# Zero products where no bank of sums is open: a graph layer on one Trainium2 core

## The chip, the cores and the metric

The kernel runs on one core of one Trainium2 chip. The core has five engines that run side by side, each through its own list of instructions in order: PE (TensorE, matmuls; its weight loads are shown as PEld), DVE (VectorE), ACT (ScalarE), POOL (GpSimd) and SP (SyncE, which here issues the transfers). Matmul results go into eight banks of PSUM, an accumulator memory that DVE and ACT read. The clock of TensorE can be granted at full speed (1.00) or less.

The metric is the device time of one execution in microseconds (us), lower is better. The time shown for a kernel is the median of its runs.

## The reference

Inputs are `x` (4096 x 64), an adjacency matrix `adj` (4096 x 4096, of 0.0 and 1.0 in float32, 64 MiB), a weight (64 x 64) and a bias (64). Cut to what is computed:

```python
h = relu(layernorm(x))
support = h @ weight
mask = adj != 0
rank = cumsum(mask, axis=1)             # how many neighbours up to here in the row
deg = rank[:, -1:]
k = minimum(deg, 100)
pos = rank - (deg - k)
w = mask * where(pos > 0, 0.5 ** (k - pos), 0)
out = x + w @ support + bias
```

For a neighbour, `k - pos` is the number of neighbours to its right in the same row. So each neighbour weighs one half to the power of that number, and only the last 100 neighbours of a row count. The work is to read 64 MiB, to count to the right in every row, to take a power and to multiply by `support`.

## The kernel before, in words

The adjacency matrix is cut into 32 tiles of 128 rows. Each tile passes through the same steps, each a small function of the kernel:

- `load` (SP, L355) brings a tile into one of four buffers `a_sb`. The first two and the last four tiles come in pieces. A buffer is free again once it is converted.
- `convert` (DVE, L563) makes bytes of the floats, and `flip` (DVE, L573) transposes in blocks of 32, so that a row's elements lie along the partitions (`mt`).
- `totals` (PE, L581) counts neighbours in blocks, into a bank. `split` (ACT, L589) takes two kinds of count out of it (`sums`). `suffix` (PE, L602) adds up the blocks to the right, into a bank. `clamp` (DVE, L608) cuts off what lies more than 100 neighbours away (`behind`).
- `place` (PE, L618 and L622) makes the count to the right of every element, into four banks at once. `weigh` (ACT, L636, four per tile) takes the power and writes the weights `wk`. In the last tiles DVE does some of this with `encode` and `take` (L643, L647).
- `aggregate` (PE, L656) multiplies the weights of two tiles with `support` (`hr`), in eight calls of four matmuls, into a part of a bank of sums. A bank of sums serves four tiles, except for the last four, whose two pairs have a bank each.
- `drain` (ACT or DVE, L671 and L673) takes a finished bank of sums and adds the bias. `turn_back` (PE, L679) transposes it back, `finish` (DVE, L685) adds `x`, and `store` (SP, L689) writes the result.

Layer norm, `support` and constants (L370 to L551) are made in the first 40 us, beside the first tiles.

**What sets the order.** All steps are made as tasks with a due time from a list written into the kernel. A function `plan` goes through them with estimated durations. It gives out the eight banks, and it returns one list of steps; every engine executes its own steps in the order of this list. For a step that needs new banks, `plan` names them, and they become the list `homes`, from which the step takes them with `bank()`. The banks 0 to 7 of the plan are called `bank` in the profile, and a step that takes a bank waits until its last reader is done with it.

**The zero products.** `plan` also returns with every step of PE a number `spare`. It estimates the time for which PE has nothing to do before the step and the matmul rows of the last 3.4 us, and from both works out how many products of zeros should be put in. The loop over the plan calls `warm(spare)` ahead of each step. `warm` (L482 to L484) makes that many matmuls of 128 x 256 zeros (`junk`). They go into the place that the list `idle` names: a bank and a column in it. At the start that is the second half of the last bank; after each `aggregate` it is the part of the bank of sums that this call added to. There the products have neither a first nor a last mark, so that zero is added to open sums. When `drain` takes that bank, `idle` is emptied. From then until the next `aggregate` in the list no bank of sums is open, and `warm` makes nothing, whatever `spare` says.

Of the kernel before, what the change touches and what calls it, by code (L numbers as in the profile page):

```python
# [118 lines left out]
def read_by(u):  # L119

    g = u // 2
    return [("drain", d) for d, (k, i0, i1, _) in enumerate(DRAINS) if k == g and (u not in ALONE or i0 == u % 2 * 2)][-1:]
# [102 lines left out]
def dma_ns(f, args):  # L225
    if f == "fetch":
        return 950
    _, k0, k1 = LOADS[args[0]]
    return (k1 - k0) * {8: 611, 4: 620, 2: 630}[k1 - k0] + (300 if args[0] == REST else 0)


def late(at):

    return 450 if at < 17000 else 1900 if at < 104000 else 3300


def rows_of(f, args):

    return {"turn": 150, "center": 2048, "support": 2048, "totals": 512, "suffix": 1408, "place": 1024, "aggregate": 1024,
            "turn_back": 2048}.get(f, 0)  # L240


def plan():

    todo, kinds = tasks(), {}
    for key, (f, args, engine, *_) in todo.items():
        kinds.setdefault((engine, f), []).append(key)
    ready, free = {None: 0}, list(FREE)
    landed, taken, order = 0, {p: [] for p in SIZES}, []
    banks = [None] * (BANKS - 1) + read_by(0)  # L250
    while kinds:
        heads = []
        for kind, keys in kinds.items():
            f, args, engine, due, hold, lag, needs, pool = todo[keys[0]]
            if pool and pool[0] in SIZES:
                needs = needs + (taken[pool[0]] + list(pool[1:]))[:-SIZES[pool[0]]][-len(pool) + 1:]
            elif pool:
                needs = needs + [k for _, _, k in sorted((ready[k], i, k) for i, k in enumerate(banks) if k in ready)][:len(pool) - 1]
                if len(needs) < len(todo[keys[0]][6]) + len(pool) - 1:
                    continue  # L260
            if all(r in ready for r in needs):
                heads.append((max([free[engine]] + [ready[r] for r in needs]), due, engine, kind))
        soon, _, engine, _ = min(heads)
        _, at, kind = min((due, at, kind) for at, due, e, kind in heads if e == engine and at <= soon + WAIT[engine])
        key = kinds[kind].pop(0)
        if not kinds[kind]:
            del kinds[kind]
        f, args, _, _, hold, lag, _, pool = todo[key]
        homes = []
        if pool and pool[0] in SIZES:  # L270
            taken[pool[0]] += pool[1:]
        elif pool:
            homes = [i for _, i in sorted((ready[k], i) for i, k in enumerate(banks) if k in ready)][:len(pool) - 1]
            for i, k in zip(homes, pool[1:]):
                banks[i] = k
        if f in ("load", "fetch"):
            lag = max(landed - at, 2450) + dma_ns(f, args)
            landed = at + lag
            lag += late(landed)
        if f in FULL:  # L280
            hold, lag = hold + 95, lag + 95
        ready[key] = at + lag + 60
        free[engine] = at + hold
        order.append((at, hold, engine, f, args, homes))
    spent, end, result = [], 1200, []
    for at, hold, engine, f, args, homes in order:
        idle = 0
        if engine == PE:
            recent = sum(rows for when, rows in spent if when > at - 3400)
            idle = max(0, min(int((at - end) * 0.6) // 110, (4200 - recent) // 256))  # L290
            spent += [(at, rows_of(f, args) + 256 * idle)]
            end = at + hold
        result.append((at, idle, f, args, homes))
    return result
# [3 lines left out]
def kernel(  # L298
# [12 lines left out]
    nc = tc.nc  # L311
    P = 128
# [21 lines left out]
    banks = [ps.tile([P, W], F32, name=f"bank{i}") for i in range(BANKS)]  # L334
    homes = []
# [35 lines left out]
    junk = setup.tile([P, 2 * P], BF16, name="junk")  # L371
# [108 lines left out]
    idle = [banks[BANKS - 1], 2 * P]  # L480

    def warm(n):  # L482
        for i in range(n if idle else 0):
            nc.tensor.matmul(idle[0][:, idle[1]:idle[1] + 2 * P], junk[:, :P], junk, start=not accs, stop=not accs, skip_group_check=True)  # L484

    pxs, ns = {}, {}

# [68 lines left out]
    masks, words, wts, accs, pts, sums8, behind, vs, codes = {}, {}, {}, {}, {}, {}, {}, {}, {}  # L556
# [130 lines left out]
    def store(s):  # L687
# [5 lines left out]
        support, scale, first, second, convert, flip, totals, split, suffix, clamp, place, weigh, encode, take, aggregate,  # L693
        drain, turn_back, finish, store)}
    for at, spare, f, args, given in plan():
        warm(spare)
        homes[:] = given
        does[f](*args)

    last = {}  # L700
# [34 lines left out]
```

## Time and profile before

| | |
|---|---|
| runs of the kernel | 185.85, 186.7 and 187.02 us; median 186.7 |
| profiled execution | 187.01 us, of which its span 185.0 us (first to last instruction) |
| PE, weight loads | 165.2 us busy (89%), 128.4 us (69%); 2087 matmuls |
| DVE | 153.9 us busy (83%) |
| ACT | 149.5 us busy (81%) |
| POOL | 7.7 us busy (4%) |
| mean granted clock of TensorE | 0.980 |
| DMA | 69.55 MB, 376 GB/s over the span |
| zero products (L484) | 93, 14.7 us busy, mean 299 ns |
| first reading of the matrix | loads (L355) issued from 1.2 to 150.9 us |

Busy time is the time in which an engine has an instruction running. Matmuls overlap: a mean of 299 ns for one does not mean that the next starts 299 ns later. In the view of 40 slices each digit is the busy share of 4.6 us in tenths, 9 for 90% or more; the row PEclk shows the granted clock in the same way. An idle time in brackets in the timeline names what the engine waited for. A wait for several things is put down to the one that came last.

### The profile page before, as it was taken

How to read it: one execution, taken by the hardware profiler on the slowest of the kernel's cores; microseconds unless marked ns; L12 is line 12 of the kernel's file. 1: busy time of each engine (PE TensorE's matmuls, PEld its weight loads, DVE VectorE, ACT ScalarE, POOL GpSimd, SP SyncE). 2: the span in 40 equal slices, each digit the busy share in tenths (PEclk: the TensorE clock that was granted, in tenths of full speed). 3: DMA queues.
4: the chain of work that ended last, by engine and by line, in shares of the span. 5: the costliest groups of instructions: out<-in, count | busy, mean ns of one | idle time of the engine just before them, and what ended most of it. 6: DMA issues, size and time to landing. Idle time of an engine off the chain costs nothing.

```text
span 185.0 us, 4842 instructions
## 1 busy us (share of the span) xinstructions
PE 165.2 (89%) x2087; PEld 128.4 (69%) x2087; DVE 153.9 (83%) x204; ACT 149.5 (81%) x196; POOL 7.7 (4%) x43
## 2 busy tenths in 40 slices
PE   7999987579799999899999899997499999989992
PEld 5857874267586776687868588776277678777891
DVE  6667299999999999898889698888984989998731
ACT  2476912839699999999999999994896999999931
POOL 7810000000000000000000000000000000000000
PEclk9999999999999999999999999999958999999999
DMA  6999999999999999999999999999999999960020
GB/s 225 420 415 436 429 425 418 441 407 446 414 436 418 427 425 418 436 429 425 425 422 432 418 429 432 418 432 425 429 422 420 413 416 416 414 267 0 4 87 28
DMA packets 6807, 69.55 MB, mean 376 GB/s; under 512 B 898, under 2 KB 1154, under 8 KB 2178
## 3 DMA queue, kind: packets, MB, share of 16 engines
q1 hardware_dynamic: 6786, 69.24, 89.1%
q8 instruction: 16, 0.26, 0.6%
q14 instruction: 5, 0.04, 0.1%
HBM read 68.19 MB, written 1.05 MB: 374 GB/s over the span
## 4 chain that ended last, share of the span: by engine, by line
ACT 29%; PE 26%; DMA 19%; DVE 16%; issue 8%; SPq 0%; ACTq 0%; DVEq 0%
ACT wk L636 23%; DMA a_sb<-in_adj_dram 19%; PE bank L656 15%; DVE m L563 8%; ACT sums L589 4%; PE bank L602 4%; DVE mt L573 3%; PE bank L679 3%; PE bank L622 2%; PE bank L581 2%; PE bank L618 2%; DVE behind L608 1%; DVE wk L532 1%; DVE hr L542 1%; ACT acc_sb L671 1%
## 5 line engine op out<-in xcount | busy, mean ns | idle before, releaser
L636 ACT ACTIVATE wk<-bank 128x1024 fp32r<-128x1024 uint8 (+2 forms) x136 | 122.7, 1067 | 7.9 <-PE bank L622 6.3
L563 DVE TENSOR_SCALAR m<-a_sb 128x2048 uint8<-128x2048 f32 (+1 forms) x66 | 85.7, 1345 | 14.5 <-DMA a_sb<-in_adj_dram 14.3
L656 PE MATMUL bank<-wk,hr 128*128 128x256 f32 x512 | 73.2, 292 | 3.5 <-DVE hr L542 2.5
L656 PEld LDWEIGHTS bank<-wk,hr 128*128 128x128 f32 x512 | 64.4, 192 | 10.3 <-issue 5.0
L573 DVE STREAM_TRANSPOSE mt<-m 128x1024 f32<-128x1024 f32 (+2 forms) x40 | 40.5, 1022 | 0.4
L589 ACT ACTIVATE sums<-bank 128x512 f16<-128x512 uint8 x32 | 21.6, 685 | 7.2 <-PE bank L581 7.2
L608 DVE TENSOR_SCALAR behind<-bank,excess 128x256 f16<-128x256 f32 x32 | 14.8, 466 | 4.4 <-PE bank L602 4.1
L602 PEld LDWEIGHTS <-far 128*128 128x128 f16 x224 | 17.7, 99 | 0.9
L602 PE MATMUL bank<-sums,far 128*128 128x224 f16 (+6 forms) x224 | 18.1, 222 | 0.0
L618 PE MATMUL bank<-behind,where 32*128 32x256 f16 x256 | 14.5, 277 | 3.9 <-DVE behind L608 1.9
L484 PE MATMUL bank<-junk 128*128 128x256 bf16 x93 | 14.7, 299 | 1.2 <-DVE junk L372 1.2
L581 PE MATMUL bank<-mt,band 128*32 128x256 f16 x256 | 13.3, 284 | 2.4 <-DVE mt L573 1.7
L622 PE MATMUL bank<-mt,tri 32*32 32x512 f16 x512 | 14.4, 403 | 0.0
L602 PE MATMUL bank<-sums,near 128*128 128x256 f16 x32 | 9.0, 280 | 4.4 <-ACT sums L589 3.8
L484 PEld LDWEIGHTS <-junk 128*128 128x128 bf16 x93 | 9.0, 106 | 4.8 <-issue 2.0
L618 PEld LDWEIGHTS <-where 32*128 32x128 f16 x256 | 4.7, 92 | 9.8 <-issue 7.4
L581 PEld LDWEIGHTS <-band 128*32 128x32 f16 x256 | 4.5, 95 | 7.9 <-issue 3.8
L622 PEld LDWEIGHTS <-tri 32*32 32x32 f16 x512 | 4.4, 88 | 6.9 <-issue 6.9
L602 PE MATMUL bank<-sums,rest 128*128 128x256 f16 x32 | 8.8, 276 | 0.0
L495 ACT ACTIVATE wk<-bank 64x512 f32<-64x512 f32 x8 | 4.3, 587 | 4.9 <-PE bank L491 4.9
L685 DVE TENSOR_TENSOR xr<-bank,xr 128x256 f32<-128x256 f32 (+1 forms) x9 | 3.5, 389 | 5.6 <-PE bank L679 5.6
L679 PE MATMUL bank<-both,acc_sb 128*128 128x64 f32 x56 | 7.5, 277 | 0.6 <-ACT acc_sb L671 0.6
(95 smaller groups left out, 86.2 us busy)
## 6 DMA issues: line engine op xcount, KB each, us to landing
a_sb<-in_adj_dram SPq DMA_DIRECT2D x26, 2048.0 KB, 16.8
a_sb<-in_adj_dram SPq DMA_DIRECT2D x10, 1024.0 KB, 12.7
a_sb<-in_adj_dram SPq DMA_DIRECT2D x4, 512.0 KB, 14.5
xr<-in_x_dram SPq DMA_DIRECT2D x2, 512.0 KB, 4.8
out_dram<-xr SPq DMA_DIRECT2D x1, 512.0 KB
out_dram<-xr SPq DMA_DIRECT2D x1, 384.0 KB, 2.7
out_dram<-xr SPq DMA_DIRECT2D x2, 64.0 KB, 1.6
w<-in_L_gnn_weight_dram SPq DMA_DIRECT2D x2, 16.0 KB, 9.4
```

Source lines behind the costliest of these rows:

```text
L484: nc.tensor.matmul(idle[0][:, idle[1]:idle[1] + 2 * P], junk[:, :P], junk, start=not accs, stop=not accs, skip_group_check=True)
L563: nc.vector.tensor_scalar(words[n][:, k0 * P:k1 * P, :].rearrange("p (h q) e -> p h e q", q=P), tiles[t][:, (h0 + k0) * W:(h0 + k1) * W].r ...
L573: nc.vector.transpose(to[:, h0:h1], m_v.rearrange("p (h c l) -> p h c l", c=4, l=SUB))
L581: nc.tensor.matmul(tot[SUB * c:SUB * (c + 1), r], band[:, SUB - 12 - 4 * a:2 * SUB - 12 - 4 * a], masks[t][:, c, r, a], start=(a == 0), st ...
L589: nc.scalar.activation(sums8[t][:, :, r], pts.pop((n, "n")).bitcast(U8).rearrange("p (i f) -> p f i", f=4)[:, :2, r], AF.Copy, bias=-136.0)
L602: nc.tensor.matmul(o, l, m, start=(k == 0), stop=(k == len(todo) - 1), skip_group_check=True)
L608: nc.vector.tensor_scalar(behind[n][:, r], pts.pop((n, "s"))[:, r], excess, float(MAX_NEIGH), op0=ALU.subtract, op1=ALU.min)
L618: nc.tensor.matmul(vs[n, j][:, h0:h1, a, :], where[q, a, :], behind[n][q, r], start=(a == 0), stop=False, skip_group_check=True)
L622: nc.tensor.matmul(vs[n, j][SUB * c:SUB * (c + 1), h0:h1], tri[q, q], masks[t][q, c, r, :].rearrange("p (h r) a -> p h a r", r=SUB), start ...
L636: nc.scalar.activation(to[:, :, :, j, :], v[:, :2, x], AF.Exp, scale=-LN2, bias=-38.0 * LN2)
L656: nc.tensor.matmul(accs[g][:, at:at + 2 * P], hr[:, h * 4 + e, :, :].rearrange("p s d -> p (s d)"), wts[u][:, s, 2 * h + a].rearrange("p i ...
L679: nc.tensor.matmul(pts["o", d][:, k, :], sums[d][:, k * P:(k + 1) * P], both, start=True, stop=True)
```

## The change

`warm` now chooses between two places. If `idle` names one, everything is as before. If `idle` is empty, and the step that comes next takes new banks, the zero products go to the first half of the first of these banks, each marked as first and last of a group of its own. The next step sets this bank anew with its own first mark. If the next step takes no bank, nothing is made. So that the banks are known, `homes` is set ahead of the call of `warm` and not behind it.

```diff
     def warm(n):
-        for i in range(n if idle else 0):
-            nc.tensor.matmul(idle[0][:, idle[1]:idle[1] + 2 * P], junk[:, :P], junk, start=not accs, stop=not accs, skip_group_check=True)
+
+        to = idle or [banks[i] for i in homes[:1]] + [0]
+        for i in range(n if len(to) > 1 else 0):
+            keep = bool(idle and accs)
+            nc.tensor.matmul(to[0][:, to[1]:to[1] + 2 * P], junk[:, :P], junk, start=not keep, stop=not keep, skip_group_check=True)
...
     for at, spare, f, args, given in plan():
+        homes[:] = given
         warm(spare)
-        homes[:] = given
         does[f](*args)
```

The three lines more ahead of it shift the line numbers behind: `warm`'s matmul stands on L487 in the changed kernel, and L581 becomes L584, L602 becomes L605 and so on.

## The prediction

> **What bounds the kernel now.** I began with the page's second part, the span in 40 slices of 4.6 us, because it shows the engines beside the clock.
>
> ```profile
> PE   7999987579799999899999899997499999989992
> DVE  6667299999999999898889698888984989998731
> ACT  2476912839699999999999999994896999999931
> PEclk9999999999999999999999999999958999999999
> DMA  6999999999999999999999999999999999960020
> ```
>
> The DMA row is full until about 165 us: reading the adjacency matrix sets the pace. VectorE (DVE) and ScalarE (ACT) stand at 8 to 9 behind it. Counting slices from 0, PE falls to 7 and 4 in slices 27 and 28 and ACT to 4 in slice 27 (125 to 129.5 us); right after, in slices 29 and 30, the granted clock shows 5 and 8. No other slice has a lower clock. So I cut this stretch into windows of 3.41 us, with one earlier window for comparison. The columns are length, then busy time and count of PE, weight load, DVE, ACT and POOL, then granted clock, DMA share and GB/s.
>
> ```profile
> 37.79:41.21 3.42, 2.08 (x18) 1.66 (x17) 3.42 (x5) 1.15 (x2) 0.00 (x0) 1.00 1.01 431
> ...
> 126.54:129.95 3.41, 2.30 (x47) 1.97 (x44) 3.41 (x5) 0.37 (x1) 0.00 (x0) 1.00 0.99 423
> 129.95:133.37 3.42, 1.36 (x48) 0.56 (x33) 3.42 (x4) 3.10 (x4) 0.00 (x0) 1.00 1.02 436
> 133.37:136.78 3.41, 3.11 (x22) 2.30 (x22) 2.84 (x4) 3.08 (x5) 0.00 (x0) 0.50 0.99 413
> 136.78:140.19 3.41, 3.41 (x34) 2.34 (x35) 1.99 (x2) 2.73 (x4) 0.00 (x0) 0.50 1.03 437
> 140.19:143.61 3.42, 3.42 (x41) 3.00 (x43) 2.25 (x3) 2.48 (x3) 0.00 (x0) 1.00 0.97 412
> ```
>
> The cuts are not arbitrary: the trace's clock record is at half from 133.37 to 140.19, 6.83 us, and two windows of 3.41 fit it. The window before the fall holds 1.36 us of PE work, the least of those I looked at. The next least after the start, 37.79 to 41.21 with 2.08 us, kept the full clock. So the trace puts the point at which the clock falls between 1.36 and 2.08 us of work in a window.
>
> Next, what PE and ACT did there, in the timeline in order of time (start, length, engine and line, and in brackets the idle time before and what ended it).
>
> ```profile
> 129.41 0.40 PE L618 MATMUL bank<-behind,where 32*128 32x256 f16 x8 [1.11 <-DVE behind L608]
> ...
> 131.35 0.41 PE L581 MATMUL bank<-mt,band 128*32 128x256 f16 x8 [0.44 <-ACT wk L636]
> 133.67 0.37 PE L602 MATMUL bank<-sums,near 128*128 128x256 f16 x1 [1.91 <-ACT sums L589]
> ```
>
> ```profile
> 136.70 0.60 ACT L589 ACTIVATE sums<-bank 128x512 f16<-128x512 uint8 x1 [0.33 <-PE bank L581]
> ...
> 139.81 2.86 ACT L636 ACTIVATE wk<-bank 128x1024 fp32r<-128x1024 uint8 x3 [0.68 <-PE bank L622]
> 143.68 0.60 ACT L589 ACTIVATE sums<-bank 128x512 f16<-128x512 uint8 x1 [1.01 <-PE bank L581]
> ```
>
> ```profile
> 136.13 2.64 DVE L563 TENSOR_SCALAR m<-a_sb 128x2048 uint8<-128x2048 f32 x2 [0.54 <-DMA a_sb<-in_adj_dram]
> 141.36 0.48 DVE L608 TENSOR_SCALAR behind<-bank,excess 128x256 f16<-128x256 f32 x1 [2.59 <-PE bank L602]
> ```
>
> PE's holes of 1.11, 0.44 and 1.91 us starve the window. Then PE works at half clock from 133.67 without a pause, ACT waits for it three times and DVE once, 2.59 us. At 136.13 DVE still waited for a load; after 141.36 it waits for no load again. The chain of waits says the same: PE from 133.67 to 143.6, ACT from there to 162.4, PE from 162.4 to 181.
>
> **What the change does.** The plan of steps is the same; nothing is removed or reordered on DVE, ACT, POOL or SP. PE's stream gets 15 pairs of weight load and matmul, and where a bank was open the same products go to the same place as before. The 15 stand at three steps of this hole: 2 ahead of the first `place` (the row at 129.41), 3 ahead of `totals` (131.35) and 10 ahead of `suffix` (133.67).
>
> *Length.* Sixteen such products back to back at 37.49 take 1.92 us and one takes 0.27, so the spacing is (1.92 - 0.27) / 15 = 0.11 us; at half clock matmuls of 256 columns are 0.213 us apart (the L656 rows at 135.2 to 135.6).
>
> *The two.* Their bank is long free. PE ends `suffix` at about 128.3 and idles 1.11 us for DVE: 2 x 0.11 = 0.22 is hidden. Cost 0.
>
> *The three.* They wait for their bank as `totals` does now (a `weigh` on ACT). `totals` starts 0.33 later, near 131.7, and ends near 132.1. Its reader `split` (L589) stands on ACT behind a `weigh` until 133.00: cost 0, with 0.9 of cover.
>
> *The ten.* They wait for the second `weigh` of that tile to free their bank; it starts at 131.19 and takes 1.02, so they run from about 132.2 to 133.3. The `suffix` behind them waits for `split` until 133.67 anyway: cost 0, with 0.36 of cover. Behind `suffix` all of PE queues; if the bank came free 0.5 later, 0.14 would be paid by everyone.
>
> *What they bring.* The window 129.95 to 133.37 would hold 1.36 + 13 x 0.11 = 2.8 us of PE work. That is above 2.08. That zero products count as work is shown by the window at 37.79: 1.62 of its 2.08 us are the same L484 products, the remaining 0.46 is far under 1.36, and the clock held. So I take the clock to stay full. The end not excluded is that it falls as before: gain 0.
>
> The Trainium skill, "TensorE: Matmul & The Clock Gate", section "Why this matters for your kernels", speaks against the change: it asks only that PE have no idle gap over some 3 us. The longest gap here is 1.91 us. By that rule the gaps did not cause the fall and filling them would leave 187.0. The trace has the clock at 0.50 right after these gaps, so I follow the windows.
>
> *What a full clock is worth.* First, on PE, by comparing rows at half clock with the same steps at full clock between 140.46 and 143.8: `suffix` 1.17 against 0.63 us, four matmuls of `aggregate` 1.13 against 0.51, `totals` 0.54 against 0.35, eight of `aggregate` 2.01 against 1.03, `place` 1.13 against 0.73, four more 0.81 against 0.51. Together 6.79 against 3.76: PE is 3.0 us earlier at 140.5. Second, ACT: from 143.68 it runs almost without a hole, so it can only win its three waits, 0.33 + 0.68 + 1.01 = 2.02 us. Third, DVE: its 2.59 us wait goes, but then it is late only by what the loads allow. The trace's completions of the loads' packets are at 141.0, 145.9, and for the last three pieces 163.3, 164.6 and 165.8; the converts of these start at 142.93, 146.98, 165.29, 166.6 and 167.81. That is late by 1.9, 1.1, 2.0, 2.0 and 2.0 us. The loads themselves cannot come earlier, the DMA share is already 0.97 to 1.03.
>
> What is late next, then, is a load: DVE waits for the one at 141.0. The load at 145.9 allows only 1.1, but DVE idles 0.90 us for PE at 149.6 before the `clamp` that follows, and this takes up the difference (1.08 + 0.90 = 1.98). The tail from 162.4 is a dense row of PE work that starts on an ACT result; it moves with ACT, and its last masks with DVE. The smallest of 3.0, 2.02 and 1.9 to 2.0 decides: **1.9 us**.
>
> **Sum.** The profiled execution took 187.01 us (span 185.0, the rest outside it). 187.01 - 1.9 + 0 = **185.1 us**. The runs shown are 185.85, 186.7 and 187.02, so the profiled one is 0.3 above their median, and 185.1 is 0.9% under the median. A difference of 1%, 1.9 us, is about what a measurement of this kernel tells from none.
>
> **Rivals.**
>
> 1. *The loads take back more.* If the 1.1 us at the load of 145.9 carries on, because the `clamp` at 150.5 still waits for its `suffix`, the gain is 1.1: 185.9. For it: the DMA row is full. Against it: DVE was 2.0 late at the last pieces, so it has that much to lose. Chance 0.17.
> 2. *PE's time counts whole.* If the tail is bound by PE alone, 3.0 us go: 184.0. For it: PE shows almost no hole from 163 to 180. Against it: PE's 0.61 us wait for ACT at 162.4. Chance 0.10.
> 3. *Nothing to win in most runs.* The windows may lie elsewhere in another run. Moved by a microsecond, the hole is split between two windows that each hold more than 1.36, and the clock may never have fallen; the run of 185.85 may be one. Or it falls in the changed kernel too. Then 186.2 to 187.0. Chance 0.13.
> 4. *Slower: the ten in the way.* If the clock is already at half when the ten run, they take 10 x 0.213 = 2.1 us, from 132.2 to 134.3, and `suffix` and all of PE behind it start 0.66 us late: 187.7. It decides from the point at which the ten end after 133.67, that is a clock that falls before about 132.9 or a bank freed after 132.57. For it: the cover is only 0.36 us. Against it: the clock was full until 133.37 without the products. Chance 0.06.
>
> **Numbers.** The forecast has 0.54, with its own range 184.6 to 185.6. Under 184.83 (1% below the median) lie the second rival and about 0.2 of the forecast: faster 0.31. Over 188.6 lies only the fourth rival with a second fall of the clock: slower 0.04. The rest, 0.65, is within 1%. The range from 184.2 to 187.0 leaves out the slow rival and part of the second.
>
> **What would show it.** Right: 108 products on L487 instead of 93 on L484; a granted clock of 1.00 from 133 to 140; PE's hole before `suffix` down from 1.91 to under 0.5; DVE's 2.59 us wait gone, and a wait for a load near 141; ACT's `split` near 141.7 instead of 143.68; the last convert near 165.9. Wrong: a clock of 0.5 anywhere after 128, `suffix` starting after 133.7, or a last convert still near 167.8.

## The result, and the profile after

The changed kernel takes 185.04 us (median of 20 executions, 184.59 to 187.22), the kernel before 186.87 us (20 executions, 185.60 to 187.72). The ratio is 0.9924, with a 95% interval of 0.9897 to 0.9951, which does not reach 1: a gain of 0.8%. The profiled execution took 184.69 us with a span of 182.7 us, against 187.01 and 185.0 before: 2.32 us less. The medians differ by 1.83, because the execution profiled before lay 0.14 over the median of its kernel and the one after 0.35 under.

First the page of the changed kernel, two rows of its 40 slices.

```profile
PE   7899987569889999899999899999699999999992
...
PEclk9999999999999999999999999999999999999998
```

Counting slices from 0, PE has none under 6 between slice 7 and the last, and the granted clock does not drop before the very end. Now the windows of 3.41 us around the hole (length, busy time and count of PE, weight load, DVE, ACT, POOL, then clock, DMA share, GB/s). In this execution their cuts lie 0.35 us later than in the one before.

```profile
130.31:133.72 3.41, 2.77 (x45) 1.64 (x45) 3.41 (x3) 3.36 (x5) 0.00 (x0) 1.00 0.97 413
133.72:137.13 3.41, 3.22 (x37) 2.41 (x36) 2.67 (x4) 3.41 (x5) 0.00 (x0) 1.00 1.02 428
```

The window of the hole holds 2.77 us of PE work instead of 1.36, and the clock stays at 1.00 behind it. The timeline of PE shows the 15 products in their places.

```profile
128.25 0.38 PE L487 MATMUL bank<-junk 128*128 128x256 bf16 x2
129.50 0.40 PE L621 MATMUL bank<-behind,where 32*128 32x256 f16 x8 [0.87 <-DVE behind L611]
...
131.44 0.49 PE L487 MATMUL bank<-junk 128*128 128x256 bf16 x3 [0.45 <-ACT wk L639]
131.86 0.41 PE L584 MATMUL bank<-mt,band 128*32 128x256 f16 x8
132.35 1.25 PE L487 MATMUL bank<-junk 128*128 128x256 bf16 x10
133.76 0.27 PE L605 MATMUL bank<-sums,near 128*128 128x256 f16 x1 [0.15 <-ACT sums L592]
...
138.11 0.28 PE L605 MATMUL bank<-sums,near 128*128 128x256 f16 x1
```

`suffix` starts at 133.76 (133.67 before; everything is 0.09 later from 129.5 on) and still waits 0.15 us for ACT. The ten fit. The last line is the `suffix` of the next tile, 24. Then ACT and DVE, from the same timeline:

```profile
136.28 0.67 ACT L592 ACTIVATE sums<-bank 128x512 f16<-128x512 uint8 x1
...
141.32 0.70 ACT L592 ACTIVATE sums<-bank 128x512 f16<-128x512 uint8 x1
```

```profile
141.10 2.66 DVE L566 TENSOR_SCALAR m<-a_sb 128x2048 uint8<-128x2048 f32 x2 [0.44 <-DMA a_sb<-in_adj_dram]
143.63 0.48 DVE L611 TENSOR_SCALAR behind<-bank,excess 128x256 f16<-128x256 f32 x1
...
166.01 0.76 DVE L566 TENSOR_SCALAR m<-a_sb 128x1024 uint8<-128x1024 f32 x1
```

ACT's three waits are gone; the `split` of tile 25, at 143.68 before, stands at 141.32. DVE waits for the load of 141.0 again, and its last convert starts at 166.01 instead of 167.81. The two lines of before for comparison, the `suffix` of tile 24 and the last convert:

```profile
140.46 0.28 PE L602 MATMUL bank<-sums,near 128*128 128x256 f16 x1
```

```profile
167.81 0.73 DVE L563 TENSOR_SCALAR m<-a_sb 128x1024 uint8<-128x1024 f32 x1
```

**Which chain set the end.** Thirteen profiles, of both kernels and of the experiments below, bear on that. For each I set the start of the `split` of tile 25 on ACT beside the span:

| profile | split of tile 25 | span | difference |
|---|---|---|---|
| before | 143.68 | 185.02 | 41.34 |
| before, once more (e5) | 143.97 | 185.28 | 41.31 |
| five products (e1) | 143.84 | 185.15 | 41.31 |
| clamp moved, no products (e9) | 143.12 | 184.40 | 41.28 |
| without the sixteen (e7) | 142.39 | 183.80 | 41.41 |
| ten behind (e3) | 142.07 | 183.41 | 41.34 |
| twenty (e4) | 141.76 | 183.10 | 41.34 |
| ten alone (e2) | 141.75 | 183.19 | 41.44 |
| after | 141.32 | 182.70 | 41.38 |
| clamp moved, with products (e8) | 141.32 | 182.74 | 41.42 |
| eight ahead of `place` (e10) | 141.33 | 182.71 | 41.38 |
| clamp moved, with products, again (e12) | 141.59 | 182.89 | 41.30 |
| after, once more (e11) | 140.93 | 182.84 | 41.91 |

Without e11 the splits spread over 2.65 us, the difference over 0.16 us. From 141 on ACT has no hole worth naming, and what it is late there it is late at the end.

The exception is e11, the changed kernel itself in a second profile. Its `split` came 0.39 us earlier than in the first, and its span was 0.14 longer. There the chain that ended last runs through a load, for which DVE waits (0.75 us at 146.01 in the first profile):

```profile
146.43 2.69 DVE L566 TENSOR_SCALAR m<-a_sb 128x2048 uint8<-128x2048 f32 x2 [1.19 <-DMA a_sb<-in_adj_dram]
```

So, as I read the table, ACT sets the end as long as it is late. The five profiles with the `split` at 141.6 or before all have a span of 182.70 to 182.89, whatever ACT gained on top: from there on the loads have a say again. The part of the clock can be read from the same profiles: the four in which it falls in the hole (before, e5, e1, e9) have spans of 184.40 to 185.28, the nine in which it does not 182.70 to 183.80.

### The profile page after: what moved, and what is told of

It is laid out like the page before. It is cut to its first block, busy times and chain, and to the rows that moved or that the text cites. A ratio compares the mean times of both kernels' runs of the same rounds, so it can differ in the third digit from the quotient of the medians.

```text
span 182.7 us, 4872 instructions
## 1 busy us (share of the span) xinstructions
PE 163.4 (89%) x2102; PEld 126.8 (69%) x2102; DVE 154.2 (84%) x204; ACT 149.0 (82%) x196; POOL 7.8 (4%) x43
## 4 chain that ended last, share of the span: by engine, by line
ACT 32%; PE 21%; DMA 19%; DVE 17%; issue 8%; SPq 0%; ACTq 0%; DVEq 0%
ACT wk L639 26%; DMA a_sb<-in_adj_dram 19%; PE bank L659 12%; DVE m L566 9%; ACT sums L592 5%; DVE mt L576 3%; PE bank L605 3%; PE bank L682 3%; PE bank L625 2%; PE bank L621 1%; DVE wk L535 1%; DVE hr L545 1%; DVE behind L611 1%; PE bank L584 1%; ACT acc_sb L674 1%
## 5 line engine op out<-in xcount | busy, mean ns | idle before, releaser
L659 PE MATMUL bank<-wk,hr 128*128 128x256 f32 x512 | 71.8, 288 | 3.4 <-DVE hr L545 2.5
L659 PEld LDWEIGHTS bank<-wk,hr 128*128 128x128 f32 x512 | 63.0, 188 | 9.8 <-issue 4.6
L487 PE MATMUL bank<-junk 128*128 128x256 bf16 x108 | 16.5, 291 | 2.1 <-DVE junk L372 1.2
L605 PEld LDWEIGHTS <-far 128*128 128x128 f16 x224 | 17.3, 98 | 0.7
L605 PE MATMUL bank<-sums,far 128*128 128x224 f16 (+6 forms) x224 | 17.7, 219 | 0.0
L584 PE MATMUL bank<-mt,band 128*32 128x256 f16 x256 | 13.1, 281 | 2.5 <-DVE mt L576 2.3
L487 PEld LDWEIGHTS <-junk 128*128 128x128 bf16 x108 | 10.3, 104 | 6.3 <-issue 3.5
L605 PE MATMUL bank<-sums,near 128*128 128x256 f16 x32 | 8.9, 277 | 2.6 <-ACT sums L592 2.0
L584 PEld LDWEIGHTS <-band 128*32 128x32 f16 x256 | 4.4, 94 | 7.9 <-issue 4.3
L605 PE MATMUL bank<-sums,rest 128*128 128x256 f16 x32 | 8.7, 272 | 0.0
```

The costliest lines, as they stand in the source:

```text
L487: nc.tensor.matmul(to[0][:, to[1]:to[1] + 2 * P], junk[:, :P], junk, start=not keep, stop=not keep, skip_group_check=True)
L584: nc.tensor.matmul(tot[SUB * c:SUB * (c + 1), r], band[:, SUB - 12 - 4 * a:2 * SUB - 12 - 4 * a], masks[t][:, c, r, a], start=(a == 0), st ...
L605: nc.tensor.matmul(o, l, m, start=(k == 0), stop=(k == len(todo) - 1), skip_group_check=True)
L659: nc.tensor.matmul(accs[g][:, at:at + 2 * P], hr[:, h * 4 + e, :, :].rearrange("p s d -> p (s d)"), wts[u][:, s, 2 * h + a].rearrange("p i ...
```

## The experiments

**Which of the 15 products are needed.** First the 2 and the 3 without the 10:

```diff
-        warm(spare)
+        warm(0 if (f, args) == ("suffix", (23,)) else spare)
```

> Only the 2 and the 3 products are made, the 10 ahead of suffix are left out. Theory (the clock falls where a window of 3.41 us holds too little PE work): the window of the hole holds 1.36 + 3 x 0.11 = 1.7 us, between the 1.36 that fell and the 2.08 that held, so this places the point: if it falls, the time is that of before, ratio 0.998 to 1.003; if it holds, the time is that of the changed kernel, ratio 0.990 to 0.994. Rival (a single gap of idle time decides): the longest gap is still about 1.4 us against 1.91, the same two outcomes; this run alone does not tell the two apart.

Measured: 186.26 us (12 executions), before 186.50 (29), ratio 0.999 (0.9964 to 1.0015). The windows of its profile:

```profile
130.73:134.14 3.41, 1.47 (x25) 1.05 (x20) 3.37 (x4) 3.41 (x5) 0.00 (x0) 1.00 1.04 442
134.14:137.55 3.41, 3.27 (x22) 2.52 (x20) 2.80 (x4) 3.31 (x5) 0.00 (x0) 0.50 0.96 404
```

The clock falls behind a window with 1.47 us of work, and nothing is gained. Then the 10 alone:

```diff
-        warm(spare)
+        warm(0 if (f, args) in {("place", (21,)), ("totals", (23,))} else spare)
```

> Only the 10 products ahead of suffix are made. Theory: the window holds 1.36 + 1.1 = 2.5 us, over 2.08, the clock stays full, and the time is that of the changed kernel: ratio to before 0.990 to 0.995, clock 1.00 from 133 to 140, no wait of DVE for PE near 141. Rival (all 15 are needed, or the gain is not from the clock): ratio 0.997 to 1.003.

Measured: 185.16 us (11 executions), ratio 0.9939 (0.9916 to 0.9962). The clock is 1.00 through the hole. The ten carry nearly all of the gain; this run does not tell whether the five add the rest. But the same profile holds a surprise at 33 us, in a stretch that the change does not touch. The first line is its hole, the other two are that stretch:

```profile
131.65:135.07 3.42, 2.43 (x27) 1.88 (x27) 3.36 (x4) 3.42 (x6) 0.00 (x0) 1.00 1.02 431
...
32.67:36.08 3.41, 2.26 (x33) 0.93 (x30) 3.41 (x3) 3.41 (x5) 0.00 (x0) 1.00 0.98 411
36.08:39.50 3.42, 2.41 (x11) 2.22 (x12) 3.42 (x6) 0.80 (x2) 0.00 (x0) 0.50 1.00 426
```

A window with 2.26 us of PE work lost the clock, though before one with 2.08 had kept it. Busy time is not what decides.

**The same number in another place.** The ten stand behind `suffix`:

```diff
-        warm(spare)
+        warm({("suffix", (23,)): 0, ("aggregate", (10, 0)): 10}.get((f, args), spare))
```

> The same 15 products, but the 10 stand behind suffix, ahead of the first aggregate of the next bank of sums, some 1 us later and outside the hole. Theory: the hole is starved as before, the clock falls near 133, the 10 run at half clock in the way of PE (10 x 0.213 = 2.1 us), ratio 1.000 to 1.012, the granted clock 0.5 for 6.8 us. Rival (the number of products or some other effect of the longer program matters, not their place): ratio 0.990 to 0.995.

Measured: 185.72 us (12 executions, 184.99 to 187.33), ratio 0.9973 (0.9943 to 1.0003). Neither theory nor rival foresaw that: four executions lie at 186.7 to 187.3 and eight at 185.0 to 185.8. The profiled one is of the eight, and it kept the clock:

```profile
128.48:131.89 3.41, 2.95 (x65) 1.64 (x64) 3.41 (x6) 1.47 (x2) 0.00 (x0) 1.00 0.98 418
131.89:135.31 3.42, 1.92 (x27) 1.59 (x27) 3.38 (x4) 3.42 (x5) 0.00 (x0) 1.00 1.05 441
```

The windows happened to part the hole: the work before 131.9 went into one, and `suffix` and eight of the ten into the next. My reading is that place matters through the windows, and that these lie differently in each execution. That the other four lost the clock in the hole is what the theory says, but no profile of one was taken. Their mean granted clocks (0.991 for the one of 186.74, 0.981 and 0.982 for the rest) leave room for 3.3 and for 6.7 to 7.0 us at half clock: enough for one fall of 6.83 us in three of them, and for a short one at most in the fourth.

**The kernel before, profiled again.** No edit.

> The kernel before, unchanged, profiled once more. Theory (the clock is decided in windows of 3.41 us that lie differently in each execution; the hole starves one of them wherever they lie, but how much of the half clock falls on waiting PE differs): the clock falls once near the hole, between 131 and 136; the time is between 185.6 and 187.8 and follows where ACT's split stands, split + 41.4 us = span, as in the profiles of before (143.68 and 185.0) and after (141.32 and 182.7). Rival (the executions near 185.7 have no fall, and the rest of the gain comes from elsewhere): a profile with full clock from 125 to 145 and a time over 185.5.

Measured: 187.26 us, `split` at 143.97, span 185.28. The fall near the hole comes at 133.31, as expected:

```profile
129.90:133.31 3.41, 1.91 (x56) 0.81 (x56) 3.41 (x5) 2.51 (x3) 0.00 (x0) 1.00 0.99 423
133.31:136.72 3.41, 2.53 (x21) 2.03 (x20) 2.84 (x4) 3.41 (x5) 0.00 (x0) 0.50 1.02 428
```

Beside the run above this is a clean pair: 1.92 us of PE work kept the clock, 1.91 us lost it. But "once" was wrong. The page of this profile has a second fall, from 34.32 to 41.15, which the first profile of the same kernel did not have (slices 7 and 8):

```profile
PEclk9999999759999999999999999999858999999999
```

The rival about the executions near 185.5 us is not settled. Seven executions of the kernel before lie under 185.75 with a clock on record. Their mean clock is 0.991 in three, 0.985 in two, and 0.979 and 0.977 in the others. That leaves room for 3.3, 5.5, and about 8 us at half clock in all. So five of them can't have had a fall of 6.83 us in the hole, the other two can, and no such execution was profiled.

**What decides instead of busy time.** I counted the columns that PE streams in a window: each matmul that starts in it with its columns (one with 128x256 has 256), and matmuls side by side in different strips of the array once (the 8 of `totals` as 2, the 8 + 16 of `place` as 2 + 1). From 25 us on, this orders all windows of the thirteen profiles that hold none of the slow float32 matmuls (those of `turn_back`, for one: 0.12 us apart with 64 columns). The clock fell at 1536 (before), 2176 (e9, at 33.28), 2304 (e3, at 32.91), 2560 (e5), 2688 (e1) and 2816 (e2, at 32.67, and e5 and e7); it held at 3072 (after, at 31.32), 3200 (before, at 27.55), 3968 (e3, at 131.89), 4096 (before, at 37.79) and 4608 (after, at 130.31). Products of zeros are dense columns, 0.11 us each for 256; `place` is long in busy time and short in columns. So in these profiles the point lies between 2816 and 3072 columns in 3.41 us, one product apart. I found this measure after the fact, among runs that were there, and no run was made to test it. In the first 25 us float32 matmuls make the count unsure.

**More products than fit.** Twenty instead of ten ahead of `suffix`:

```diff
-        warm(spare)
+        warm(20 if (f, args) == ("suffix", (23,)) else spare)
```

> 20 products instead of 10 ahead of suffix. Theory: the clock stays full; the ten more take 1.1 us, of which 0.15 us are covered by the wait for split, so suffix starts 0.95 us later, near 134.7; ACT's next two splits wait for PE, 0.4 us each; ratio to before 0.993 to 0.998, that is 0.4 to 0.9 us over the changed kernel. Rival (PE has enough slack behind the hole): ratio as the changed kernel's, 0.990 to 0.993.

Measured: 185.08 us (7 executions), ratio 0.9932 (0.9906 to 0.9959). In its profile, PE and then ACT:

```profile
132.32 2.34 PE L487 MATMUL bank<-junk 128*128 128x256 bf16 x20
134.50 0.27 PE L605 MATMUL bank<-sums,near 128*128 128x256 f16 x1
```

```profile
136.30 0.61 ACT L592 ACTIVATE sums<-bank 128x512 f16<-128x512 uint8 x1
...
141.76 0.60 ACT L592 ACTIVATE sums<-bank 128x512 f16<-128x512 uint8 x1 [0.26 <-PE bank L584]
```

`suffix` starts 0.74 us later than in the changed kernel, where 0.95 was expected. Only one of the two splits waits, and it stands 0.44 later; the span is 0.40 longer. The medians of the two kernels cannot tell this apart, and single executions of the changed kernel differ by more: their spans lie between 182.6 and 183.3, but for the three longest.

**A fall elsewhere.** The changed kernel without the 16 zero products ahead of an early `aggregate`:

```diff
-        warm(spare)
+        warm(0 if (f, args) == ("aggregate", (0, 2)) else spare)
```

> The changed kernel without the 16 zero products ahead of the third aggregate call, at 37.5 us. Theory (zero products count as PE work, and the price of a fall depends on what PE holds up): the window there is left with about 0.5 us of work, the clock falls near 40 in every execution for 3.4 to 6.8 us; DVE is busy without a pause there, PE has slack, and loads are ahead by four buffers, so the time is that of the changed kernel within 0.4 us: ratio 0.990 to 0.996. Rival (a fall costs 2 us wherever it is): ratio 1.000 to 1.005. Rival (zero products do not count): no fall near 40.

Measured: 185.49 us (10 executions), ratio 0.9935 (0.9909 to 0.9961), inside the ratio expected, while the 0.45 over the changed kernel is just beyond the 0.4. The profile is of the longest of the ten (185.81). In it the clock had already fallen at 33.44, behind a window that the edit leaves as it was. It then stays down for four windows, not one or two, and the window without the 16 is the second of them:

```profile
33.44:36.85 3.41, 3.02 (x29) 1.55 (x29) 3.19 (x4) 2.47 (x4) 0.00 (x0) 0.50 1.05 447
36.85:40.27 3.42, 1.37 (x7) 1.07 (x6) 3.13 (x4) 1.15 (x2) 0.00 (x0) 0.50 0.97 412
40.27:43.68 3.41, 2.68 (x12) 2.68 (x13) 3.41 (x5) 2.04 (x4) 0.00 (x0) 0.50 1.03 437
43.68:47.10 3.42, 3.42 (x22) 2.73 (x20) 3.42 (x4) 2.31 (x3) 0.00 (x0) 0.50 1.00 426
```

13.7 us at half clock leave a span of 183.8, 1.1 over the changed kernel's; 6.8 us in the hole cost 2.3. So the price of a fall does not follow from its length. That it is set by what waits for PE there is my reading, from one profile of each. In e2, two windows at half clock here and one near 19 went with a span of 183.2.

**A shorter hole.** DVE's `clamp` of tile 21 is moved ahead of the second `convert` of tile 23, for which it waits 1.3 us. Once with the new products (e8), once without (e9):

```diff
+    steps = plan()
+    names = [(s[2], s[3]) for s in steps]
+    steps.insert(names.index(("convert", (25, 1))), steps.pop(names.index(("clamp", (21,)))))
-    for at, spare, f, args, given in plan():
+    for at, spare, f, args, given in steps:
```

> The changed kernel, with DVE's clamp of tile 21 moved ahead of the second convert of tile 23, so that the first place need not wait for this convert (1.3 us). Theory (behind the hole ACT's chain to the end is set from 133 on by totals that wait for flips that wait for loads): ACT restarts 1.1 us earlier, near 129.2, but the split of tile 25 only 0.2 us earlier; ratio 0.990 to 0.993, as the changed kernel. Rival (the hole's length itself sets the end): 1.1 us less than the changed kernel, ratio 0.985 to 0.988.

Measured: 184.83 us (5 executions), ratio 0.9909 (0.9873 to 0.9945). ACT in its profile:

```profile
129.77 2.86 ACT L639 ACTIVATE wk<-bank 128x1024 fp32r<-128x1024 uint8 x3 [2.35 <-PE bank L625]
...
141.32 0.60 ACT L592 ACTIVATE sums<-bank 128x512 f16<-128x512 uint8 x1 [0.37 <-PE bank L584]
```

ACT restarts 0.59 earlier than in the changed kernel (130.36), not 1.1, and not all of that need come from the move: in e11, without it, ACT restarts at 129.91. But the `split` of tile 25 stands at the same 141.32, now with a wait of 0.37 for `totals`, which in turn waits 0.21 for a flip on DVE. This flip follows a convert that waited 1.17 us for its load. The loads have the say again, and the end is the same.

> The kernel before, without the new products, with the same move of the clamp. PE's hole then ends about 1.1 us earlier, at suffix near 132.5, and is shorter. Theory (work in a window decides): fewer positions of the windows starve; where the clock holds the time is 185.0, where it falls 186 to 187; ratio between 0.993 and 1.000. Rival (only zero products help): ratio 0.998 to 1.004.

Measured: 186.48 us (10 executions), ratio 1.0002 (0.9962 to 1.0042). The profiled window from 128.85 to 132.27 holds 2560 columns:

```profile
128.85:132.27 3.42, 2.02 (x60) 0.84 (x58) 3.41 (x5) 2.50 (x3) 0.00 (x0) 1.00 1.03 441
132.27:135.68 3.41, 2.37 (x13) 2.01 (x14) 3.38 (x4) 3.41 (x5) 0.00 (x0) 0.50 1.02 428
```

`suffix` stands at 133.17, not near 132.5. A shorter hole alone does not keep the clock in this profile, nor bring the time down. One execution of the ten took 184.87, the others 186.05 and more. My upper end of 1.000 is just what came out; that fewer window positions starve did not show.

**Eight instead of two ahead of `place`.** Three of the 20 executions of the changed kernel took 186.8 to 187.2 us. This run was to show whether a window cut at 128.8 is the cause.

```diff
-        warm(spare)
+        warm(8 if (f, args) == ("place", (21,)) else spare)
```

> The changed kernel with 8 zero products instead of 2 ahead of the first place. The 6 more take 0.66 us of the 0.87 us that PE still idles there, so they delay nothing. Theory (a few executions of the changed kernel, 186.8 to 187.2 us, have their windows cut so that the one from about 128.8 to 132.2 starves; the ten then run at half clock): with 1536 more columns in that window no execution is over 185.8; median 184.7 to 185.2, ratio to before 0.989 to 0.993. Rival (these executions lose their time in the first 45 us): the same share of them, some 1 in 7, stays near 187.

> The changed kernel, unchanged, beside the others of this call on the same chip. Ratio to before 0.990 to 0.995, and about 1 execution in 7 near 187.

> The changed kernel with DVE's clamp of tile 21 moved ahead of the second convert of tile 23, once more, beside the changed kernel itself. If the hole sets nothing but the clock, its median is that of the changed kernel within 0.2 us, ratio to before 0.990 to 0.993. If the earlier restart of ACT carries to the end, it is over 0.5 us faster than the changed kernel.

Measured side by side, six executions each: eight products 185.00 us (ratio 0.9922, 0.9900 to 0.9945), the changed kernel 184.91 (0.9921, 0.9898 to 0.9945), the changed kernel with the moved clamp 184.82 (0.9918, 0.9893 to 0.9943). None of the 18 lies over 185.3. So the three versions are not told apart, the moved clamp brings nothing that carries to the end, and the cause of the three long executions stays open: none came up here. What is on record of them is a mean granted clock of 0.959, some 15 us at half clock, against at most 11 us in the other 17 of the changed kernel. So they lost the clock for longer than the others; where, it does not say.

## Why the prediction was right, and where its working was not

The forecast of 185.1 us stands against a median of 185.04, and the profiled execution, at 184.69, gained 2.32 where 1.9 was forecast. That the median came so near is partly luck: the gain forecast was 0.4 short of that between the profiles, and the execution profiled after happened to lie 0.35 under its median, which made up for most of it.

- **The clock.** Right. It stays at 1.00 through the hole; e1 and e5 show that it falls there where the ten are missing, and e2 that the ten alone keep it. Of the three holes named as starving the window, the one of 1.11 us ended at 129.41, before the window began; 0.44 and most of 1.91 lie in it. The step that named the point "between 1.36 and 2.08 us of work in a window" was wrong: 1.92 kept the clock and 2.26 lost it. What the runs put in its place is 2816 to 3072 columns. The conclusion survived because products of zeros are dense: by columns too, 1536 and 13 products of 256 are far above the point.
- **The rule weighed against it.** The Trainium skill, "TensorE: Matmul & The Clock Gate", section "Why this matters for your kernels", asks for no idle gaps over some 3 us. In e1 the longest gap of PE in the hole was 1.50 us, and the clock fell. Here the rule is too mild.
- **Length and cover of the products.** Right: the ten take 1.25 us with the last one's end, `suffix` waits 0.15 more for ACT, and `totals` at 131.86 is well ahead of `split` at 133.09.
- **What a full clock is worth on PE.** 3.0 us was too much: the `suffix` of tile 24 moved from 140.46 to 138.11, 2.35 us. From one `suffix` to the next PE took 4.35 us, not 3.76. In that stretch a weight load waits 0.26 us for ACT's `weigh` at 134.68, and the three groups of `aggregate` take 0.34 more than the rows that the sum used.
- **On ACT.** The mechanism was right and the term too small: 2.02 was the sum of the three waits, and 2.36 came (143.68 to 141.32). A `weigh` lasts 1.02 us or more, but the next step on ACT starts 0.90 behind it when nothing holds it up. So each wait that goes also gives back an overlap: the three steps in which ACT had waited shrank by 0.51, 0.81 and 1.10, 2.42 in all, and ACT's start 0.09 later took some of it back.
- **The smallest decides.** The cap was put in the wrong place. DVE's last convert moved by 1.80, and the end by 2.32 all the same: how late DVE's last converts are does not bound the gain. The end followed ACT. That loads cap it is right all the same, only later: the table shows no span under 182.70, however early ACT's `split`, and in e11 the chain runs through the load that landed at 146.4. What came as forecast is that DVE waits for the load at 141.
- **Rival 1**, that the load at 145.9 keeps the gain to 1.1: it fell, DVE's `clamp` at 148.59 follows its convert without a wait, and even where this load is in the chain (e11) the span is 2.2 shorter than before. **Rival 2**, PE's time counts whole: it fell with the 2.35. **Rival 3**: executions of the kernel before near 185.5 do exist, so there is little to win in some; whether they kept the clock is open, and so is whether the place of the windows makes the difference. **Rival 4**, the ten in the way: e4 puts the price of a late `suffix` at 0.40 us for 0.74, by one profile of each. Three executions of the changed kernel at 187 would fit ten products at half clock, but no profile shows it.

## What to carry to other kernels

When the granted clock drops, cut the profile into windows that fit the drop, and look for the starved window ahead of it, not for the longest gap; count dense matmul columns rather than busy time, which misjudged windows here. Then ask who waits for PE during the drop: half clock cost 2.3 us for 6.8 us where ACT's chain to the end hung on PE, and about 1.1 us for 13.7 us near 40 us, by one profile. Products of zeros that wait for the same bank as the next step are free as long as they end before that step's other input arrives, and it is that margin, here 0.15 us, that has to be worked out.

## What the runs showed of the hardware that was not expected

In these profiles the clock fell where fewer than some 2,900 columns (2816 fell, 3072 held) were streamed in 3.41 us; by my estimate 31 products of 256 columns, 0.11 us apart, would fill such a window with 7936. What brings it back is less clear. Behind the hole, windows with 3200 (before) and 3072 columns (e1) were followed by another at half clock, those with 3328 (before) and 3488 (e1) by full clock, though one with 3072 (e5) was followed by full clock as well, so this order is not sharp. And the windows have no fixed place against the kernel's work: three profiles without the ten products show the fall at 133.31, 133.37 and 134.14, while `suffix` starts at 134.19, 133.67 and 133.50. One with the moved clamp shows it at 132.27. This may be why executions of one and the same kernel differ by 2 us; no run here shows that it is.
